# Metaformer on one NeuronCore: 87 of 4608 gathered rows are fetched by SyncE, position by position

## The chip, the cores and the metric

The kernel runs on one core of a Trainium2 chip. The metric is the device time of one execution in microseconds (us), lower is better. The engines are named as the profile names them: PE is TensorE (PEld its weight loads), DVE is VectorE, ACT is ScalarE, POOL is GpSimd, and SP is SyncE, which computes nothing and issues most of the DMAs. SPq stands for SyncE's queue.

## The reference

Four images of 128 channels and 128 x 128 pixels pass two layers. What matters here is the first one, a deformable 3 x 3 convolution. For each pixel and each of the nine taps, an offset is computed by an ordinary convolution, and the image is sampled bilinearly at the shifted place:

```python
g = jax.vmap(lambda img, yy, xx: img[:, yy, xx])(x, iyc, ixc)
return g * (w * valid.astype(x.dtype))[:, None]
...
return corner(y0, x0, wy0 * wx0) + corner(y0, x1, wy0 * wx1) + corner(y1, x0, wy1 * wx0) + corner(y1, x1, wy1 * wx1)
```

`x` is the image after a normalisation over its channels. The samples are weighted with `w_conv` and summed over the taps. After it come, for each pixel, a mixture of the two best of eight experts, a channel mixing that equals the reference's Fourier layer, and a layer of 64 experts that takes eight tokens each from an image.

## The kernel before, in words

**The table.** For each image the kernel writes a table into the device memory (`Image.table`): for each pixel of the padded image the 128 normalised channels of the pixel and of the one below it, 256 float32. Two neighbouring entries, 2 KB, hold the four corners of a sample. `positions` computes for each pixel and tap the entry's number (`Image.index`, one per partition, where the partition is the pixel's column x) and the four corner weights (`Image.weight`).

**Chunks.** A group is four image rows (`row_groups`), and a `Chunk` is one tap of a group: 4 rows x 128 pixels. There are 32 groups x 9 taps x 4 images = 1152 chunks. `Chunk.gather` issues one indirect DMA on GpSimd for each of the four rows; it brings 128 entries of 2 KB onto 128 partitions, into the tile `g` (six buffers, `AHEAD`). `weighted` multiplies three of the rows by their corner weights on VectorE in one instruction (all four rows for tap 0), `weighted_too` does the fourth on ScalarE with four activations, `summed` adds the four corners by 16 accumulating transposes on TensorE into `trg`, and `moved` copies the result to `sT` on ScalarE. `Group.convolved` multiplies `sT` with the convolution's weights into `sums`, and `mixed` does what follows for the group (experts, mixing, gates).

**The order.** A loop over `n` at the end of the kernel walks the chunks. Each chunk has two half steps ("slots"); `Turns` holds jobs (Python generators) that are resumed in those slots, so that the work of other stages is laid between the chunks. The order in which the loop records instructions is the order on each engine (`InOrder`, the helper whose line the profile shows as L104 for nearly everything). After `summed` of chunk n, the gathers of chunk n + 6 are issued. The table and positions of image b + 1 are made by jobs during the chunks of image b: `block` (transposes, normalisation, the store of the table), `padding` (a transpose and a copy into one of four buffers `pads`), `offsets` (six matmuls on two padded buffers), `positions`.

**SyncE's queue** holds the loads and stores in the order of recording: `xc` (image rows), `table<-ent` (the table's blocks), `xg` (the residual's rows of a group), `x_d<-x` (the group's result), and from the fourth image on the expert weights and the output of the first three images. A DMA's waits hold back all that stands behind it on the queue.

**Memory.** From the fourth image on, buffers that are no longer needed take expert weights: `rooms` lists among others `flat_pads`, the four padded buffers. `blank` is a block of zeros that a matmul with `iota` uses to clear `sums`.

Of the kernel before, what the change touches and what calls it, by code (L numbers as in the profile page):

```python
# [42 lines left out]
F32 = mybir.dt.float32  # L43
I32 = mybir.dt.int32
U32 = mybir.dt.uint32
AF = mybir.ActivationFunctionType
ALU = mybir.AluOpType
AX = mybir.AxisListType
# [3 lines left out]
P = 128  # L52
# [5 lines left out]
HID = 512  # L58
# [6 lines left out]
TAPS = 9  # L65
EPS_C = 1e-6
EPS_T = 1e-5
RB = 8
CB = 16
TW = P + 1  # L70
TC = P + 2
# [14 lines left out]
BANKS = 6  # L86
AFTER = 11
SPACE = 13
BLOCK = 84
FILL = "fill"  # L90
DONE = "done"
# [98 lines left out]
def metaformer_kernel(  # L190
# [50 lines left out]
    with ExitStack() as main:  # L241
# [91 lines left out]
        for pad in pads:  # L333
            nc.vector.memset(pad, 0.0)
        flat_pads = [pad.rearrange("p y x -> p (y x)")[:, 0:HID].unsqueeze(1) for pad in pads]
        aT_sb = wts.tile([P, P], F32, name="aT_sb")

        gwT_sb = wts.tile([P, 2 * E1], F32, name="gwT_sb")
        gb_sb = wts.tile([P, 1], F32, name="gb_sb")


        blank = wts.tile([P, P], F32, name="blank")
        nc.vector.memset(blank, 0.0)
        flip = wts.tile([P, P], F32, name="flip")
        nc.gpsimd.memset(flip, 0.0)
        for base in (0, -P):
# [108 lines left out]
                yield from with_bias(ew_sb[:, 4 * h : 4 * h + 4, :], biases[h])  # L455


        def padding(t, h, row, read, padded):

            yield FILL  # L460
            tr = transposes(row, 4)
            read.append(h)
            yield turns.hop
            eng.scalar.copy(pads[(2 * t + h) % 4][:, :, 1 : P + 1], tr)
            padded.append(h)

        def offsets(im, t, padded):

            while len(padded) < 2:
                yield 1  # L470
            yield 1


            yield FILL
            po = bank([P, 4, P], "po")
            for k in range(3):
                for h in range(2):
                    eng.tensor.matmul(
                        po[h * P // 2 : (h + 1) * P // 2],
                        lhsT=woff_sb[:, k, :],  # L480
                        rhs=pads[(2 * t + h) % 4][:, :, k : k + P],
                        start=(k == 0),
                        stop=(k == 2),
                    )
            yield turns.hop
# [13 lines left out]
            yield turns.hop  # L499
            if i0 == 0:  # L500
                im.z[q] = pa.tile([P, CB + 2, 6 * TAPS], F32, name=f"z{im.b}_{q}", tag="z")
                if q == 0:
                    eng.vector.memset(im.z[q][:, 0, :], 0.0)
                else:
                    eng.scalar.copy(im.z[q - 1][:, CB + 1, :], tr[:, 0, 0, 0 : 6 * TAPS])
            eng.scalar.copy(
                im.z[q][:, 1 + i0 : 1 + i0 + RB, :].rearrange("p (h i) o -> p h i o", h=2),
                tr[:, :, :, 0 : 6 * TAPS].rearrange("p i h o -> p h i o"),
            )
            if i0 == 0 and q > 0:  # L510
# [192 lines left out]
        class Group:  # L703
# [30 lines left out]
            def convolved(self, k):  # L734

                yield 1
                if k + 1 < FIRST:
                    return
                if k + 1 == FIRST:
                    eng.tensor.matmul(  # L740
                        sums.rearrange("p s c -> p (s c)"),
                        lhsT=blank,
                        rhs=iota,
                        start=True,
                        stop=False,
                    )
# [13 lines left out]
                if k + 1 == TAPS:  # L760
                    yield turns.hop
                    yield from mixed(self)

        class Chunk:


            def __init__(self, group, k):
                self.group, self.k = group, k
                self.shared = k > 0

            def gather(self):
                self.g = pg.tile([P, 4, 4, P], F32, name="g", tag="g")
                im = self.group.im
                for s, y in enumerate(self.group.rows):
                    eng.gpsimd.indirect_dma_start(
                        out=self.g[:, s].rearrange("p v c -> p (v c)"),
                        out_offset=None,
                        in_=im.table,
                        in_offset=bass.IndirectOffsetOnAxis(
                            ap=im.index[:, y, self.k : self.k + 1], axis=0  # L780
                        ),
                    )

            def weighted(self):
                n = 3 if self.shared else 4
# [4 lines left out]
                )  # L790

            def weighted_too(self):
                g, y = self.g[:, 3], self.group.rows[3]
                w = self.group.im.weight[y // CB]
                for v in range(4):
                    eng.scalar.activation(
                        g[:, v, :], g[:, v, :], AF.Copy, scale=w[:, y % CB, self.k, v : v + 1]
                    )

            def summed(self):  # L800

                self.tr = bank([P, 4, P], "trg")
                for s in range(4):
                    for v in range(4):
                        eng.tensor.matmul(
                            self.tr[:, s, :],
                            lhsT=self.g[:, s, v, :],
                            rhs=ident,
                            is_transpose=True,
                            start=(v == 0),  # L810
                            stop=(v == 3),
                        )

            def moved(self):
# [2 lines left out]
                eng.scalar.copy(group.sT[self.k], self.tr)  # L817
                turns.start(group.convolved(self.k))


        exps = []

# [766 lines left out]

        def in_turn():  # L1590

            for b in range(NB):
                for number, (rows_of, minus, runs) in enumerate(orders[b]):
                    im = images[b]
                    if im.sent <= P // RB or not im.weight.keys() >= {y // CB for y in rows_of}:
                        raise ValueError("a table is late")
                    group = Group(images[b], number, rows_of, minus, runs)
                    group.begin()
                    for k in range(TAPS):
                        chunk = Chunk(group, k)  # L1600
                        chunk.gather()
                        yield chunk

        source = in_turn()
        chunk = [next(source) for _ in range(AHEAD)]
        turns.hop = HOP
# [5 lines left out]
        def tick(more):  # L1612

            turns.fills(0)
            turns.slot += 1
            if more and total - QUICK <= n <= total:
                turns.steps()
                turns.fills(0)
                turns.slot += 1

        while n < total + 3 or turns.jobs:
# [134 lines left out]
```

## Time and profile before

| | |
|---|---|
| median of 14 runs | 6119.08 us (6113.19 to 6127.06) |
| the profiled execution | 6122.13 us, of which the trace's span is 6120.4 us |
| granted clock of TensorE, mean | 0.96 |
| first and last gather start | 119.9 us and 5927.3 us |
| busy: PE, PEld, DVE, ACT, POOL | 5442.7, 4446.7, 4842.3, 3819.6, 4467.1 us |
| DMA: mean rate; share of GpSimd's queue, of SyncE's and ScalarE's | 249 GB/s; 64.7%, 14.2% |
| DMAs of SyncE | 687 |

Busy time counts what an engine executes; registers, waits and the issuing of DMAs on SyncE are not counted. A gather on GpSimd counts as busy while GpSimd makes its descriptors. In a line of the timeline stand the start in us from the span's start, the duration in us, the engine, the source line, the operation, the tile written and the tiles read, the count, and in brackets the idle time before it with what ended it. In a line of the waits stand the total in us, how often, and the longest.

### The profile page before, as it was taken

The page shows a single profiled execution, that of the slowest core. Times are in us where ns is not written, and L with a number is a line of the kernel's source. Part 1 is how long each engine was busy: PE and PEld are TensorE (multiplying, and loading weights), DVE is VectorE, ACT ScalarE, POOL GpSimd, SP SyncE. Part 2 cuts the span into 40 slices and gives each one's busy share as a digit, 9 for nine tenths or more (in the row PEclk, how much of TensorE's full clock was granted, in tenths as well). Part 3 has the DMA queues.
Part 4 walks back from the last instruction along what each step waited for, and adds up shares of the span by engine and source line. Part 5 has one row for each costly group of instructions (what it writes and reads, how often), then busy time and mean ns, then how long its engine had stood idle before and what let it go on. Part 6 is the DMA issues. An engine that isn't in the chain of part 4 may idle for free.

```text
span 6120.4 us, 118020 instructions
## 1 busy us (share of the span) xinstructions
PE 5442.7 (89%) x38823; PEld 4446.7 (73%) x38823; DVE 4842.3 (79%) x15420; ACT 3819.6 (62%) x9910; POOL 4467.1 (73%) x4795
## 2 busy tenths in 40 slices
PE   6899999998899999989889999999888898999984
PEld 4777777777777777777777777777677687777763
DVE  5678888887788888888778888888788787888872
ACT  4567666665666666666666666666555565666652
POOL 5777777777777777777777777777777777777750
PEclk8999999999999999999999999999999999999997
DMA  7778787877777877877777777778777897998777
GB/s 235 227 238 257 240 254 243 253 236 224 240 242 241 248 241 246 250 234 225 231 246 245 242 242 248 238 245 249 222 225 215 293 339 218 323 337 312 225 226 277
DMA packets 579234, 1526.15 MB, mean 249 GB/s; under 512 B 86456, under 2 KB 225408, under 8 KB 578624
## 3 DMA queue, kind: packets, MB, share of 16 engines
q0 software_dynamic: 369664, 1210.35, 64.7%
q1 hardware_dynamic: 206656, 299.87, 14.2%
q8 instruction: 310, 5.08, 0.3%
q10 hardware_dynamic: 2304, 8.39, 0.3%
q14 instruction: 300, 2.46, 0.1%
HBM read 1381.43 MB, written 136.85 MB: 248 GB/s over the span
## 4 chain that ended last, share of the span: by engine, by line
PE 33%; DMA 25%; DVE 15%; ACT 10%; POOL 9%; issue 8%; DVEq 0%; POOLq 0%; ACTq 0%; SPq 0%
DMA g<-table,index 22%; PE trg L104 11%; PE sums L104 9%; POOL g L104 9%; PE pe L104 6%; DVE g L104 6%; DVE x L104 4%; ACT g L104 4%; PE po L104 2%; DMA out<-w 2%; PE tr L104 2%; ACT sT L104 1%; ACT xn L104 1%; ACT L104 1%; PE small L104 1%
## 5 line engine op out<-in xcount | busy, mean ns | idle before, releaser
L104 POOL DMA_INDIRECT g<-table,index x4608 | 4367.8, 948 | 1416.1 <-issue 984.2
L104 DVE TENSOR_TENSOR g<-g,small 128x1536 f32<-128x1536 f32 (+1 forms) x1152 | 2081.8, 1808 | 881.2 <-DMA g<-table,index 762.0
L104 PE MATMUL trg<-ident,g 128*128 128x128 f32 x18432 | 2274.8, 278 | 158.4 <-DVE g L104 61.2
L104 PEld LDWEIGHTS trg<-ident,g 128*128 128x128 f32 x18432 | 2108.5, 144 | 279.4 <-DVE g L104 66.8
L104 ACT ACTIVATE g<-g,weight 128x128 f32<-128x128 f32 x4096 | 1306.1, 391 | 813.2 <-DMA g<-table,index 804.6
L104 DVE SCALAR_TENSOR_TENSOR x<-pe,gate,x 128x128 f32<-128x128 f32 x4072 | 1384.2, 341 | 102.2 <-PE pe L104 49.1
L104 PEld LDWEIGHTS sums<-wconv_sb,sT 128*128 128x128 f32 x9216 | 1139.1, 194 | 339.6 <-ACT sT L104 185.0
L104 PE MATMUL sums<-wconv_sb,sT 128*128 128x128 f32 x9216 | 1214.1, 280 | 139.1 <-ACT sT L104 138.2
L104 PE MATMUL pe<-ew_sb,nT 128*128 128x512 f32 x2048 | 1053.3, 613 | 168.7 <-ACT sT L104 145.2
L104 ACT COPY sT<-trg 128x512 f32<-128x512 f32 x1152 | 653.4, 568 | 115.3 <-PE trg L104 114.9
L104 PEld LDWEIGHTS pe<-ew_sb,nT 128*128 128x128 f32 x2048 | 332.3, 195 | 340.2 <-ACT sT L104 197.7
L104 ACT ACT_TABLE_LOAD x263 | 337.4, 1283 | 7.5 <-DVE nmax L104 2.2
L104 ACT ACTIVATE xn<-x,c_nb,c_rs 128x128 f32<-128x128 f32 x512 | 211.3, 485 | 163.0 <-DVE c_nb L104 163.0
L104 ACT ACTIVATE n<-x,b_nb,b_rs 128x128 f32<-128x128 f32 x512 | 210.3, 482 | 131.1 <-DVE b_nb L104 64.3
L104 ACT ACTIVATE c_rs<-c_mv,eps_c 128x4 f32<-128x4 f32 x128 | 37.9, 296 | 401.9 <-DVE c_mv L104 398.7
L104 ACT ACTIVATE tn<-x,d_nb,d_rs 128x128 f32<-128x128 f32 x512 | 210.9, 483 | 73.8 <-DVE d_nb L104 73.8
L104 PE MATMUL po<-pad,woff_sb 128*64 128x512 f32 x768 | 193.7, 623 | 24.0 <-DVE x L104 21.0
L104 PEld LDWEIGHTS sums<-ident,xg 128*128 128x128 f32 x1024 | 147.9, 208 | 74.0 <-issue 74.0
L104 ACT ACTIVATE ent<-raw,a_nb,a_rs 128x128 f32<-128x128 f32 x384 | 157.9, 484 | 15.9 <-DVE a_nb L104 14.0
L104 PEld LDWEIGHTS ps<-aT_sb,xfT 128*128 128x128 f32 x1024 | 131.5, 199 | 46.3 <-ACT xfT L104 38.1
L104 PE MATMUL ps<-aT_sb,xfT 128*128 128x128 f32 x1024 | 143.9, 285 | 20.8 <-ACT xfT L104 20.1
L104 PE MATMUL sums<-iota,blank 128*128 128x512 f32 x256 | 151.8, 679 | 0.0
(236 smaller groups left out, 5108.5 us busy)
## 6 DMA issues: line engine op xcount, KB each, us to landing
g<-table,index POOLq DMA_INDIRECT x4608, 3.8
table<-ent SPq DMA_DIRECT2D x48, 1024.0 KB, 6.4
xc<-in_x SPq DMA_DIRECT2D x64, 512.0 KB, 8.8
w<-x_d SPq DMA_DIRECT2D x64, 512.0 KB, 6.2
xg<-in_x SPq DMA_DIRECT2D x124, 256.0 KB, 6.9
x_d<-x SPq DMA_DIRECT2D x124, 256.0 KB, 4.2
out<-w SPq DMA_DIRECT2D x48, 512.0 KB, 7.0
w<-in_weight SPq DMA_DIRECT2D x42, 512.0 KB, 7.6
```

The costliest lines, as they stand in the source:

```text
L104: return self.tc.keep_in_program_order(issue(*args, **kwargs))
```

## The change

One row in each thirteen chunks is no longer gathered by GpSimd. `Lone` picks chunks (never tap 0) in advance, one after the other, and has the fourth row of each fetched by SyncE: 128 DMAs of 2 KB, one for each position, whose source address comes from a register. To get there, VectorE multiplies the row's 128 entry numbers by 1024 (bytes), TensorE transposes them onto one partition into a free corner of the PSUM tile `small`, VectorE copies them as integers to a place in SBUF, and SyncE loads 16 of them at a time into registers. Five DMAs are recorded in each half step, 26 half steps for a row; the next row follows at once. 87 rows are taken this way in the whole kernel. The chunk that uses a row stands so that nine half steps lie between the row's last DMAs and its use. `weighted_too` and `summed` then read the fetched row in place of the fourth part of `g`.

The rows land in two of the four padded buffers (`apart`). So `padding` and `offsets` use only the other two once the main loop runs, with a flag `busy` for each, and in `rooms` two spare tiles of the weights' pool stand in for these two buffers. `blank` is dropped for a part of `zeros`.

```diff
+RUN = 13
...
+        apart = [
+            pad.rearrange("p y x -> p (y x)")[:, 0:HID].rearrange("p (v c) -> p v c", c=P)
+            for pad in pads[2:]
+        ]
+        busy = [False, False]
+        lined = wts.tile([1, P], I32, name="lined")
...
-        blank = wts.tile([P, P], F32, name="blank")
-        nc.vector.memset(blank, 0.0)
...
+        def pad_of(t, h):
+            return pads[(2 * t + h) % 4 if turns.hop == 1 else h]
+
         def padding(t, h, row, read, padded):
 
+            while turns.hop > 1 and busy[h]:
+                yield 1
+            busy[h] = True
             yield FILL
...
-            eng.scalar.copy(pads[(2 * t + h) % 4][:, :, 1 : P + 1], tr)
+            eng.scalar.copy(pad_of(t, h)[:, :, 1 : P + 1], tr)
...
-                        lhsT=blank,
+                        lhsT=zeros[:, 0:P],
...
             def gather(self):
                 self.g = pg.tile([P, 4, 4, P], F32, name="g", tag="g")
                 im = self.group.im
                 for s, y in enumerate(self.group.rows):
+                    if s == 3 and self.lone is not None:
+                        continue
                     eng.gpsimd.indirect_dma_start(
...
+        class Lone:
...
+            def look(self, t):
+
+                i, begin = len(self.users), max(t + 16, self.end)
+                n = (begin + 2 * RUN + 9) // 2 + 1
+                n += n % TAPS == 0
...
+                self.users.append(n)
+                self.tiles[n] = apart[i % 2]
+                self.end = begin + 2 * RUN
+                self.ahead = self.job(i, n, im, im.index[:, y, k : k + 1], begin)
+
+            def job(self, i, n, im, index, begin):
+                places, scaled = self.places[i % 2], bx_i.bitcast(F32)[:, i % 2, 0:1]
+                eng.vector.tensor_scalar(scaled, index, 8.0 * P, None, ALU.mult)
+                yield
+                yield
+                eng.tensor.transpose(small[0:1, HID - P : HID], scaled, ident)
+                yield
+                eng.vector.tensor_copy(places, small[0:1, HID - P : HID])
+                while self.now < begin:
+                    yield
...
+                for p in range(P):
+                    if p % 16 == 0:
+                        loads, values = nc.values_load_multi_w_load_instructions(
+                            places[:, p : p + 16],
+                            engines=[mybir.EngineType.SP],
...
+                    eng.sync.dma_start(
+                        out=apart[i % 2][p : p + 1]
+                        .rearrange("p (h v) c -> p h (v c)", h=2)
+                        .bitcast(U8),
+                        in_=flat[bass.ds(values[p % 16], 16 * P)]
+                        .rearrange("(o h c) -> o h c", o=1, h=2),
+                    )
+                    if p % (P // (2 * RUN) + 1) == P // (2 * RUN):
+                        yield
...
                         chunk = Chunk(group, k)
+                        chunk.lone = lone.tiles.get(n)
+                        n += 1
                         chunk.gather()
...
                 chunk[n].summed()
                 turns.fill()
+                lone.turn(2 * n)
...
             turns.steps()
+            if 0 <= n < total:
+                lone.turn(2 * n + 1)
...
-                rooms = [[part(), part()], [part(), part()], flat_pads]
+                rooms = [[part(), part()], [part(), part()], flat_pads[0:2]]
+                rooms[-1] += [spare(), spare()]
```

More of the change, by code (lines that the diff above doesn't have):

```diff
@@ L45 @@
 U32 = mybir.dt.uint32
+U8 = mybir.dt.uint8
 AF = mybir.ActivationFunctionType
@@ L480, in offsets @@
                         lhsT=woff_sb[:, k, :],
-                        rhs=pads[(2 * t + h) % 4][:, :, k : k + P],
+                        rhs=pad_of(t, h)[:, :, k : k + P],
                         start=(k == 0),
@@ L484, in offsets @@
                     )
+            busy[:] = [False, False]
             yield turns.hop
@@ L769, in __init__ @@
                 self.shared = k > 0
+                self.lone = None
             def gather(self):
@@ L782, in gather, with last @@
                     )
+            def last(self):
+                return self.g[:, 3] if self.lone is None else self.lone
             def weighted(self):
@@ L792, in weighted_too @@
             def weighted_too(self):
-                g, y = self.g[:, 3], self.group.rows[3]
+                g, y = self.last(), self.group.rows[3]
                 w = self.group.im.weight[y // CB]
@@ L803, in summed @@
                 for s in range(4):
+                    g = self.g[:, s] if s < 3 else self.last()
                     for v in range(4):
@@ L806, in summed @@
                             self.tr[:, s, :],
-                            lhsT=self.g[:, s, v, :],
+                            lhsT=g[:, v, :],
                             rhs=ident,
@@ L818, in moved, with __init__, turn @@
                 turns.start(group.convolved(self.k))
+        class Lone:
+            def __init__(self):
+                self.places = [lined, by_i.rearrange("p y a b -> p (y a b)")[0:1, 0:P]]
+                self.tiles, self.users, self.end = {}, [], 0
+                self.ahead = self.filling = None
+                self.values = []
+            def look(self, t):
+                i, begin = len(self.users), max(t + 16, self.end)
+                n = (begin + 2 * RUN + 9) // 2 + 1
+                n += n % TAPS == 0
+                b, k = divmod(n, slots)
+                number, k = divmod(k, TAPS)
+                if n >= total or b not in images or i > 1 and begin <= 2 * self.users[-2]:
+                    return
+                im, y = images[b], orders[b][number][0][3]
+                if im.sent <= P // RB or im.known <= y // CB:
+                    return
+                self.users.append(n)
[12 more added lines that the diff above has]
+                    yield
+                self.filling, self.ahead = self.ahead, None
+                flat = im.table.rearrange("e c -> (e c)").bitcast(U8)
+                values = []
+                for p in range(P):
[3 more added lines that the diff above has]
+                            engines=[mybir.EngineType.SP],
+                            min_val=0,
+                            max_val=8 * P * (TW * TC - 2),
+                            skip_runtime_bounds_check_because="positions are clamped to the table",
+                        )
+                        for load in loads:
+                            tc.keep_in_program_order(load)
+                    eng.sync.dma_start(
[4 more added lines that the diff above has]
+                        .rearrange("(o h c) -> o h c", o=1, h=2),
+                    )
+                    if p % (P // (2 * RUN) + 1) == P // (2 * RUN):
+                        yield
+                if self.now >= 2 * n - 2:
+                    raise ValueError("a row is late")
+            def turn(self, t):
+                self.now = t
+                if self.filling is not None and next(self.filling, DONE) is DONE:
+                    self.filling = None
+                if self.ahead is None:
+                    self.look(t)
+                if self.ahead is not None:
+                    next(self.ahead)
@@ L1590, in in_turn @@
         def in_turn():
+            n = 0
             for b in range(NB):
@@ L1600, in in_turn @@
                         chunk = Chunk(group, k)
+                        chunk.lone = lone.tiles.get(n)
+                        n += 1
                         chunk.gather()
                         yield chunk
+        lone = Lone()
         source = in_turn()
@@ L1653, in metaformer_kernel @@
                 part = lambda: late.tile([P, 2, HID], F32, name="w", tag="w", bufs=4)
-                rooms = [[part(), part()], [part(), part()], flat_pads]
+                spare = lambda: pw.tile(
+                    [P, 1, HID], F32, name="w", tag="weight", bufs=3 * P // CB // 2
+                )
+                rooms = [[part(), part()], [part(), part()], flat_pads[0:2]]
+                rooms[-1] += [spare(), spare()]
                 rooms.append([pw.tile([P, 2, HID], F32, name="w", tag="index")])
```

## The prediction

> **What bounds the kernel now.** I read the page first (busy times, then the costliest groups), then GpSimd's timeline, the waits, the busy times by stage, and last the SyncE queue's timeline and the tile views. The page, part 1 and the first line of part 5:
>
> ```profile
> PE 5442.7 (89%) x38823; PEld 4446.7 (73%) x38823; DVE 4842.3 (79%) x15420; ACT 3819.6 (62%) x9910; POOL 4467.1 (73%) x4795
> ...
> L104 POOL DMA_INDIRECT g<-table,index x4608 | 4367.8, 948 | 1416.1 <-issue 984.2
> ```
>
> By busy share TensorE looks like the bound and GpSimd (POOL) looks a quarter idle. The group's line says otherwise: busy and idle time together are 5783.9 us for 4608 gathers, 1.255 us each, and most of that idle time waits for nothing that the profile shows. GpSimd's timeline in mid-kernel:
>
> ```profile
> 2998.30 0.95 POOL L104 DMA_INDIRECT g<-table,index  x1 [0.30 <-issue]
> 2999.55 0.95 POOL L104 DMA_INDIRECT g<-table,index  x1 [0.30 <-issue]
> 3000.80 0.94 POOL L104 DMA_INDIRECT g<-table,index  x1 [0.30 <-PE pe L104]
> 3002.05 0.95 POOL L104 DMA_INDIRECT g<-table,index  x1 [0.30 <-DMA g<-table,index]
> ```
>
> The starts stand 1.25 us apart, whatever releaser is named: 0.95 us of work and 0.30 us before the next one. GpSimd issues gathers without a break, four to a chunk, so a chunk takes 5.02 us. The consumers wait for it:
>
> ```profile
> ACT g L104 <- DMA g<-table,index: 804.6, 448, 19.2
> DVE g L104 <- DMA g<-table,index: 762.0, 455, 14.7
> ```
>
> And the busy times by stage (PE, PEld, DVE, ACT, POOL) show who is next:
>
> ```profile
> 300.00:4400.00 4100.00, 3739.86 (x26268) 3061.17 (x26267) 3363.39 (x10892) 2703.62 (x7056) 3102.61 (x3275) 0.97 0.79 242
> 4400.00:5930.00 1530.00, 1379.27 (x10209) 1152.78 (x10209) 1228.62 (x3600) 916.48 (x2368) 1153.63 (x1217) 0.96 0.83 271
> ```
>
> 3275 gathers in 4100 us is 1.252 us each: the gathers set this stage. TensorE is busy 91% of it, VectorE 82%.
>
> **Part one, what is removed.** 87 of 4608 gathers leave GpSimd: 87 x 1.255 = 109 us. They come out of the bound, nearly evenly (one in each 13 chunks, 1131 chunks of 1152), so all of it can be had if nothing else sets the pace. TensorE would then stand at about 91% x 5784 / 5675 = 93%, still below its limit. The profiled execution took 6122.13 us (its span is 6120.4), 3 us above the median of the runs. The gain alone gives 6122 - 109 = 6013.
>
> **Part two, what is added on SyncE.** Each of the 87 rows becomes 128 DMAs of 2 KB, which is 11136 DMAs on a queue that issued 687, and eight register loads of 16 positions. The order of the changed program shows 87 x 8 = 696 such loads, no other new work between the DMAs, and one of eight completion semaphores, in rotation, that each DMA waits for: the DMA eight places before must have landed. The rows follow each other without a gap, so SyncE must do a row, and all that it did before, in the time of 13 chunks. That is 52 x 1.255 = 65.3 us at the pace of before and 51 x 1.255 = 64.0 us with the gain. This budget decides. What one DMA costs on SyncE is read in its timeline, first near 338 us, then near 56 us and 5994 us:
>
> ```profile
> 337.37 0.37 SPq L104 DMA_DIRECT2D x_d<-x  x1
> 337.79 1.14 SPq L104 DMA_DIRECT2D table<-zeros  x2
> 338.97 0.96 SPq L104 DMA_DIRECT2D xc<-in_x  x2
> ...
> 55.65 0.53 SPq L104 DMA_DIRECT2D gb_sb<-in_gate_b  x1
> 56.23 0.58 SPq L104 DMA_DIRECT2D gwT_sb<-in_gate_w  x1
> ...
> 5993.84 5.83 SPq L104 DMA_DIRECT2D w<-in_weight  x9
> ```
>
> A DMA that stands alone takes 0.33 to 0.37 us. DMAs back to back take more: the pair of table<-zeros 1.14 us, or 0.57 each, the xc pair 0.48 each, start to start about 0.05 more. The pair of zeros is the nearest row, because its second DMA is the only 2 KB transfer of two 1 KB pieces in this kernel; the tile view gives that one 0.62 us (461 is its larger partner):
>
> ```profile
> L104 SPq DMA_DIRECT2D table<-zeros x2: 461/542/624, 337.8 to 338.3; - x2
> ```
>
> So the issue is bounded by 0.33 + 0.05 = 0.38 us and 0.62 + 0.05 = 0.67 us. The second bound on a DMA is its landing, as eight are in flight: the fastest landing in the views of SyncE's loads and stores is 3.1 us, the gathers' median 3.8, the table's zeros 5.6, so 0.39, 0.48 or 0.70 us for each.
>
> ```profile
> g<-table,index POOLq DMA_INDIRECT x4608, 3.8
> DMA to landing us min/median/max: 3.1/4.3/7.3
> ```
>
> (The second line is from the tile view of x_d.) I take 0.55 us a DMA: above the 0.48 of large DMAs back to back, below the 0.67 of the same shape, because part of that one's time may come from the 256 KB transfer just ahead of it. A register address was never used on this queue; it can add and hardly save. Of a register load no row exists. Bounds are nothing and, if it took as long as the fastest landing, 3.1 us; I take 0.5, one more instruction of the size of an isolated or a back-to-back DMA. SyncE's other DMAs between the first and the last gather are 549 in 1152 chunks, 6.2 in 13 chunks, at 0.45 us.
>
> A row: 128 x 0.55 + 8 x 0.5 + 6.2 x 0.45 = 70.4 + 4.0 + 2.8 = 77.2 us, against 65.3. SyncE becomes the bound and each row costs 11.9 us: 87 x 11.9 = +1035 us, and GpSimd's 109 us are lost in its new idle time. 6122 + 1035 = 7157 in the profile's terms, 7155 by the median.
>
> The Trainium skill bears on the one price that has no row. "Runtime: NRT & Kernel Launch", section "Instruction fetch mechanics", puts such a register load at about 200 ns for each register, even in bulk. That would be an estimate of 8 x 16 x 0.2 = 25.6 us a row in place of 4.0, and about 9035 us in all; "DMA: Bandwidth & Descriptors", section "Latency and other measured facts", has only a floor of some 600 ns for a load, with which nothing changes. No run here shows which it is.
>
> The landings above are 3.1 us and more, for transfers of 192 KB and up. "DMA: Bandwidth & Descriptors", section "Anatomy of one DMA — SWDGE (gpsimd) path", has a fit with a fixed part near 2.0 us for a DMA issued by GpSimd; with that for a small DMA of SyncE, eight in flight would allow 0.25 us each, and the limit would vanish behind the issue. No row of this trace shows a landing so short.
>
> **Part three, the small edits.** A row's indices cost one VectorE scaling, one 128x128 TensorE transpose and one copy: 87 x about 0.17 us (the timeline's reciprocal of four columns), 87 x 0.28 (the mean of the trg transposes) and 87 x at most 0.3 (a statistics instruction on 128x128 takes 0.29), 25 us for TensorE and 41 for VectorE, beside 9% and 18% idle time; without that cover the price would be at most 65 us. The clearing matmul reads another block of zeros: same size, no cost. Two buffers instead of four for the padded rows serialise a pair with its offset matmuls; the pairs come some 13 or more half chunks apart, so I price it at nothing, and at one ACT copy of 0.6 us a pair if not covered (64 pairs, 38 us). Behind SyncE's new waits stand its table stores, x_d stores, image loads and xg loads; they are asked for a group or more ahead of their use (a group is 45 us), so lateness of a few us is harmless, and a row itself has nine half chunks, 22 us, between its last DMA and ScalarE's scaling. A queue that is overloaded on the average uses this up in the second row. The fetched row's consumer is the same four ACT operations as before; they, and TensorE's transposes behind them, are who waits.
>
> **The rivals.**
> 1. *SyncE keeps up and GpSimd's gain arrives.* One condition: a position costs less than (64.0 - 4.0 - 2.8) / 128 = 0.447 us. For it speak the 0.33 us of isolated DMAs, and only two descriptors instead of 128 behind each; against it, every back-to-back row above. Time: 6013, faster by 1.8%.
> 2. *Landing decides, and with a long latency.* The 2 KB DMAs sit on the same queue behind 512 KB and 1 MB transfers and beside gathers that hold the DMA engines 79% busy. At 5.6 us, 0.70 us each: 89.6 + 4.0 + 2.8 = 96.4 us a row, 6122 + 87 x 31.1 = 8828.
> 3. *Nothing moves.* SyncE needs just about 65 us, or TensorE at 93% with its bursts takes over what GpSimd gives. Time: about 6119.
>
> **How the numbers follow.** SyncE bound by issue: 0.50. Its own range goes from 0.48 us a DMA (68.2 us a row, 6375) to 0.67 (92.6 us, 8497). Landing decides: 0.14, above that. The gain arrives: 0.32, from 6005 (the runs of before scatter by 6 to 8 us) to 6100. Nothing moves: 0.04. The range that holds 8 in 10 must span both sides and leaves out only the 0.14: 6005 to 8500. What a measurement of this kernel can tell from no change is about 0.2%, 12 us; so faster 0.32, same 0.04, slower 0.64.
>
> **What the profile after will show.** If the forecast is right, SyncE's timeline is one unbroken run of pad<-table DMAs with starts 0.5 us or more apart; GpSimd's gathers, 4521 of them, keep 0.95 us but show idle time for free g buffers; ScalarE waits for DMA pad<-table; and TensorE's busy share falls to some 76%. If rival 1 is right, SyncE shows gaps at its other waits, gathers still start every 1.25 us, and ACT's waits name g, not pad. If rival 2 is right, SyncE's DMAs are short (below 0.45 us) with waits for DMA pad<-table between them, and landings stand above 5 us. A DMA on SyncE below 0.44 us with its share of the register loads would make the prediction wrong.

## The result, and the profile after

The change makes the kernel slower, by much less than predicted. The median is 6201.99 us (6195.76 to 6207.91) against 6118.99 us: +83.0 us, a ratio of 1.0136, interval 1.0126 to 1.0146. Predicted was 7155 us, so the direction came out as forecast and the size was more than twelve times too large. The profiled execution took 6197.98 us (its span is 6196.2), 75.9 us more than that of before.

The page after, first line of part 1 and first line of part 5. The helper that records the instructions now stands at L106:

```profile
PE 5476.3 (88%) x38910; PEld 4463.3 (72%) x38910; DVE 4855.6 (78%) x15593; ACT 3814.7 (62%) x9910; POOL 4386.0 (71%) x4708
...
L106 POOL DMA_INDIRECT g<-table,index x4521 | 4287.3, 948 | 1568.9 <-issue 1066.9
```

The 87 gathers have left GpSimd and a gather still takes 948 ns, but its idle time has grown from 1416.1 to 1568.9 us. 152.8 us more idle less 80.5 us less busy is about the whole loss. The waits of the whole kernel name the same releasers as before, and shorter:

```profile
ACT g L106 <- DMA g<-table,index: 578.1, 324, 19.2
DVE g L106 <- DMA g<-table,index: 556.2, 358, 14.8
```

ScalarE waited 804.6 us for gathers and now 578.1. No wait for `DMA pad<-table` is among the long ones: the fetched rows themselves are hardly ever waited for. GpSimd's timeline in mid-kernel shows the old period of 1.25 us:

```profile
2998.23 0.95 POOL L106 DMA_INDIRECT g<-table,index  x1 [0.30 <-issue]
2999.48 0.95 POOL L106 DMA_INDIRECT g<-table,index  x1 [0.30 <-DVE a_mv L106]
3000.74 0.95 POOL L106 DMA_INDIRECT g<-table,index  x1 [0.31 <-issue]
```

So mid-kernel the bound is where it was, with fewer gathers in it. Where the loss lies shows when the same chunks are compared in both traces. The start of a chunk is here the start of VectorE's weighting of it, in us; the last two columns are two experiments that follow below, as differences to the same kernel before.

| chunk | before | after | difference | half pace | quarter transfers |
|---|---|---|---|---|---|
| 0 | 128 | 128 | +0.3 | -0.2 | +0.5 |
| 480 | 2534 | 2491 | -43.1 | -44.8 | -44.3 |
| 864 | 4459 | 4379 | -80.7 | -82.0 | -80.5 |
| 912 | 4713 | 4631 | -82.0 | -84.6 | -81.0 |
| 960 | 4956 | 4898 | -57.7 | -85.9 | -84.4 |
| 1008 | 5213 | 5205 | -8.1 | -80.7 | -80.1 |
| 1056 | 5454 | 5506 | +51.4 | -82.0 | -72.2 |
| 1104 | 5703 | 5780 | +77.8 | -92.8 | -75.1 |
| 1151 | 5931 | 6006 | +74.8 | -93.6 | -77.7 |

Two kernels in one. Up to chunk 864, 65 of the rows bring 80.7 us, 1.24 us each, as GpSimd's period says. Between chunks 912 and 1104, 159.8 us are lost, and after that nothing. The windows of before and of after for those stages (columns: window, length; busy time and count of PE, PEld, DVE, ACT, POOL; granted clock, DMA share, GB/s), before first:

```profile
4713.00:5703.00 990.00, 907.23 (x6948) 759.35 (x6947) 789.17 (x2302) 599.41 (x1541) 744.34 (x786) 0.97 0.88 298
```

```profile
300.00:4380.00 4080.00, 3770.69 (x26717) 3095.51 (x26716) 3417.57 (x11139) 2731.13 (x7142) 3087.23 (x3257) 0.98 0.80 246
4631.00:5780.00 1149.00, 961.89 (x6964) 787.34 (x6962) 790.65 (x2329) 599.37 (x1540) 729.62 (x771) 0.92 0.79 256
```

The same 192 chunks took 990 us and now 1149. VectorE, ScalarE and GpSimd do the same work in both (789 and 791, 599 and 599, 744 and 730 us), the DMA engines' share even falls, 0.88 to 0.79. Only TensorE is busy for longer, 962 us for 907, at a granted clock of 0.92 for 0.97, but over a smaller share of the stretch (84% for 92%). So something waits.

SyncE is what has changed. The tile view of `pad` and the view of the line that loads registers (columns: count, duration min/median/max in ns, first and last start in us, number of forms):

```profile
L106 SPq MOVE pad<-table x11136: 29/29/43, 140.2 to 5952.7; - x199
L106 SPq DMA_DIRECT2D pad<-table x11136: 217/228/1518, 140.3 to 5952.7; - x199
```

```profile
L883 SPq TENSOR_LOAD <-lined x352: 1147/1237/3923, 138.9 to 5943.2; - x176
L883 SPq TENSOR_LOAD <-by_i x344: 1137/1238/4092, 201.6 to 5888.4; - x172
```

A position costs 0.228 us of DMA and 0.029 of a register move; the median from start to start is 0.323 us. Sixteen registers cost 1.24 us. SyncE's timeline in the third image (start, duration, x count of a run; register loads aren't shown in it):

```profile
3006.05 20.15 SPq L106 DMA_DIRECT2D pad<-table  x40
3026.41 0.41 SPq L106 DMA_DIRECT2D xg<-in_x  x1
3026.92 6.14 SPq L106 DMA_DIRECT2D pad<-table  x15
3033.24 0.39 SPq L106 DMA_DIRECT2D x_d<-x  x1
```

Forty positions in 20.15 us are 0.50 us each, with register loads and waits in between. Added up over rows from the trace, in us for one row from its start to the next one's (positions: their DMAs, moves and the gaps below 0.15 us; waits: all longer gaps; two of the lines are of experiments that follow below):

| rows | positions | loads | other DMAs | waits | a row | budget |
|---|---|---|---|---|---|---|
| forecast | 70.4 | 4.0 | 2.8 | 0 | 77.2 | 65.3 |
| after, rows 5 to 61 | 44.3 | 10.9 | 1.9 | 6.7 | 63.9 | 64.0 |
| twelve chunks a row, rows 10 to 64 | 44.3 | 10.5 | 1.7 | 5.3 | 61.8 | 60.2 |
| after, rows 71 to 82 | 44.7 | 10.8 | 6.6 | 19.1 | 81.4 | 67.0 |
| quarter transfers, rows 71 to 82 | 44.0 | 10.2 | 6.8 | 7.9 | 69.1 | 67.0 |

In the first three images SyncE keeps step with the chunks, and issues a row's last DMA 21 us before its use on the average (rows 5 to 61). The budget of 64.0 us is 51 gathers, the pace with the gain; 60.2 is 48 gathers, the pace of before, and the budget of the rows 71 to 82 is the pace of before in that stage, 990 / 192 x 13 = 67.0 us.

SyncE's waits (total, times, longest) in the first three images, then in the stretch that loses:

```profile
SPq L106 <- DMA pad<-table: 117.2, 326, 1.2
SPq L106 <- DMA xc<-in_x: 80.2, 47, 3.5
SPq L106 <- DMA xg<-in_x: 64.1, 60, 2.3
SPq L106 <- DMA x_d<-x: 49.7, 50, 2.3
SPq L106 <- DMA table<-ent: 35.6, 28, 3.2
```

```profile
SPq L106 <- DMA w<-in_weight: 82.5, 55, 3.7
SPq L106 <- DMA w<-x_d: 76.5, 44, 3.9
SPq L106 <- DMA out<-w: 25.0, 23, 2.3
SPq L106 <- DMA pad<-table: 21.9, 64, 0.9
```

In the kernel before, SyncE waited in that stretch mostly for engines, for these two longest:

```profile
SPq L104 <- DVE x L104: 227.0, 8, 47.7
SPq L104 <- PE pf L104: 165.9, 17, 33.9
```

Added up over the whole view, SyncE waited there for engines in 726 of the 990 us. In the change it waits for engines in 45 of the 1149 us, and for landings in 234. Slower engines, TensorE with its lower clock included, would show as waits of SyncE for them; it is SyncE that now sets the pace of this stretch.

In the fourth image SyncE also loads the expert weights and `x_d` for the output of the first three images, and stores that output: 16.5 other DMAs a row (rows 71 to 82), where there were 4.6. By the table a row takes 17.5 us more than in the first three images: 4.7 for issuing those DMAs and 12.4 in waits, and the fence of the stretch that loses names their landings. Two of them in SyncE's timeline:

```profile
5209.69 0.35 SPq L106 DMA_DIRECT2D w<-x_d  x1
5210.15 4.00 SPq L106 DMA_DIRECT2D pad<-table  x5
5214.24 0.35 SPq L106 DMA_DIRECT2D w<-x_d  x1
5214.70 7.23 SPq L106 DMA_DIRECT2D pad<-table  x13
```

The last thirteen positions take 7.23 us, where 0.323 us each would be 4.2, and no register load lies among them. In the trace two of the thirteen wait, 1.5 and 1.6 us, for the landings of the two `w<-x_d` above. The fetched rows themselves are hardly late: the last DMA of the rows 71 to 73 is issued 2 to 3 us before its use, but that of the rows 75 to 82 11 to 24 us. It is what stands among them that comes late. Who waits for the late queue in that stretch (after):

```profile
POOL g L106 <- issue: 238.5, 560, 10.0
ACT w L106 <- DMA out<-w: 125.1, 25, 7.8
DVE w L106 <- DMA out<-w: 69.2, 16, 8.1
```

ScalarE and VectorE stand in front of `w` tiles whose store has not landed (ScalarE's wait of this kind was 42.0 us in the kernel before), the chunks recorded behind run late, and GpSimd issues its gathers late: its `issue` time was 170.5 us in the same stage of before. No single wait carries the loss. In the chain of waits from 4600 to 5700 us SyncE's work stands in many places: `w<-in_weight` 8.0%, `w<-x_d` 7.9%, `pad<-table` 7.4%, SyncE's own issuing 6.7%, `out<-w` 6.6%.

### The profile page after: what moved, and what is told of

It reads as the page before. It is cut to its first block, busy times and chain, and to the rows that moved or that the text cites. A ratio compares the mean times of both kernels' runs of the same rounds, so it can differ in the third digit from the quotient of the medians.

```text
span 6196.2 us, 141180 instructions
## 1 busy us (share of the span) xinstructions
PE 5476.3 (88%) x38910; PEld 4463.3 (72%) x38910; DVE 4855.6 (78%) x15593; ACT 3814.7 (62%) x9910; POOL 4386.0 (71%) x4708
## 4 chain that ended last, share of the span: by engine, by line
PE 31%; DMA 24%; DVE 17%; ACT 9%; issue 8%; POOL 7%; SPq 3%; DVEq 0%; ACTq 0%; POOLq 0%
DMA g<-table,index 16%; PE trg L106 10%; PE sums L106 9%; POOL g L106 7%; DVE g L106 6%; PE pe L106 6%; DVE x L106 4%; ACT g L106 3%; SPq L106 2%; PE po L106 2%; DMA pad<-table 2%; DMA w<-in_weight 2%; PE tr L106 2%; DMA w<-x_d 2%; DMA out<-w 1%
## 5 line engine op out<-in xcount | busy, mean ns | idle before, releaser
L106 POOL DMA_INDIRECT g<-table,index x4521 | 4287.3, 948 | 1568.9 <-issue 1066.9
L106 DVE TENSOR_TENSOR g<-g,small 128x1536 f32<-128x1536 f32 (+1 forms) x1152 | 2081.6, 1808 | 791.8 <-DMA g<-table,index 556.2
L106 PE MATMUL trg<-ident,g 128*128 128x128 f32 x18084 | 2229.1, 278 | 134.0 <-DVE g L106 45.2
L106 PEld LDWEIGHTS trg<-ident,g 128*128 128x128 f32 x18084 | 2070.7, 144 | 245.4 <-issue 86.2
L106 ACT ACTIVATE g<-g,weight 128x128 f32<-128x128 f32 x3748 | 1194.7, 391 | 622.5 <-DMA g<-table,index 578.1
L106 DVE SCALAR_TENSOR_TENSOR x<-pe,gate,x 128x128 f32<-128x128 f32 x4072 | 1383.7, 341 | 128.4 <-PE pe L106 76.2
L106 PEld LDWEIGHTS sums<-wconv_sb,sT 128*128 128x128 f32 x9216 | 1143.5, 195 | 296.5 <-issue 149.8
L106 PE MATMUL sums<-wconv_sb,sT 128*128 128x128 f32 x9216 | 1216.4, 280 | 96.3 <-ACT sT L106 95.5
L106 PE MATMUL pe<-ew_sb,nT 128*128 128x512 f32 x2048 | 1051.5, 612 | 149.7 <-ACT sT L106 95.2
L106 ACT COPY sT<-trg 128x512 f32<-128x512 f32 x1152 | 652.8, 568 | 136.2 <-PE trg L106 135.3
L106 PEld LDWEIGHTS pe<-ew_sb,nT 128*128 128x128 f32 x2048 | 331.2, 194 | 317.9 <-ACT sT L106 133.3
L106 ACT ACTIVATE xn<-x,c_nb,c_rs 128x128 f32<-128x128 f32 x512 | 211.2, 485 | 156.2 <-DVE c_nb L106 156.0
L106 ACT ACTIVATE n<-x,b_nb,b_rs 128x128 f32<-128x128 f32 x512 | 210.3, 482 | 120.2 <-DVE b_nb L106 60.6
L106 ACT ACTIVATE c_rs<-c_mv,eps_c 128x4 f32<-128x4 f32 x128 | 37.9, 296 | 391.7 <-DVE c_mv L106 376.6
L106 ACT ACTIVATE tn<-x,d_nb,d_rs 128x128 f32<-128x128 f32 x512 | 210.9, 483 | 80.0 <-DVE d_nb L106 79.7
L106 PEld LDWEIGHTS sums<-ident,xg 128*128 128x128 f32 x1024 | 148.5, 209 | 73.3 <-issue 66.1
L106 PE MATMUL po<-pad,woff_sb 128*64 128x512 f32 x768 | 190.5, 613 | 8.5 <-ACT sT L106 4.7
L106 ACT COPY w<-pf 128x512 f32<-128x512 f32 x64 | 37.1, 585 | 222.7 <-DMA out<-w 131.8
L106 ACT ACTIVATE ent<-raw,a_nb,a_rs 128x128 f32<-128x128 f32 x384 | 158.0, 484 | 20.1 <-DVE a_nb L106 18.4
L106 PEld LDWEIGHTS ps<-aT_sb,xfT 128*128 128x128 f32 x1024 | 132.0, 200 | 48.4 <-ACT xfT L106 33.8
L106 PE MATMUL ps<-aT_sb,xfT 128*128 128x128 f32 x1024 | 145.2, 287 | 24.5 <-ACT xfT L106 18.0
```

Source lines behind the costliest of these rows:

```text
L106: return self.tc.keep_in_program_order(issue(*args, **kwargs))
```

## The experiments

Three theories for the 160 us lost in the fourth image: **Q**, SyncE's queue falls behind there; **D**, the 2 KB transfers disturb the DMA engines; **R**, the buffers that the fetched rows took away from the expert weights (`rooms`, `pads`) cost it. The time before in these comparisons is 6117.61 us for the first four, 6120.28 for the next four, and 6119.02 for the last three.

**No rows in the fourth image.** 65 rows instead of 87, all memory edits kept.

```diff
-                if n >= total or b not in images or ...
+                if n >= LATE * slots or b not in images or ...
```

> The change with fetched rows only for chunks of the first three images: 65 rows instead of 87, every other edit kept (two spare tiles in rooms, two padded buffers instead of four). Theory Q (in the fourth image SyncE also issues expert weights and output tiles, its queue overflows, and what stands behind it comes late): the fourth image costs again what it cost before, and 65 x 1.255 = 82 us of gathers are gained: 6037 us. Rival R (it is the memory edits, the spare tiles and the two padded buffers that are missing, which delay the expert weights): the fourth image stays about 155 us longer than before, 6190 us. Rival D (the 2 KB transfers hold up the large ones on the DMA engines): 6037 us too; another run tells it from Q.

6043.16 us, ratio 0.9877 (0.9860 to 0.9893). The 74 us won in three images stay, so R falls: with the same buffers and no fetches there is no loss. Each row is worth 74.5 / 65 = 1.15 us.

**A pause only in the busy stretch.** 73 rows.

```diff
+                if 2 * 905 <= begin < 2 * 1085:
+                    return
```

> The change with no fetch begun in chunks 905 to 1085, where the trace of the change shows 10 to 26 other DMAs of SyncE beside each row: 73 rows. Theory Q and rival D: 73 x 1.255 = 92 us gained, 6027 us. Rival R: about 6180 us. If the rows at both ends of the fourth image cost something as well, it comes out slower than 6037 us, the time expected of the kernel without any row in the fourth image.

6038.10 us, 0.9869 (0.9853 to 0.9886), 11 us above the number expected, and about the 6043.16 us of the kernel without rows in the fourth image: the eight rows before and after the stretch cost nothing that can be measured.

**128 bytes a position.** All 87 rows and all their DMAs, a sixteenth of the data.

```diff
-                        out=apart[i % 2][p : p + 1]
-                        .rearrange("p (h v) c -> p h (v c)", h=2)
-                        .bitcast(U8),
-                        in_=flat[bass.ds(values[p % 16], 16 * P)]
-                        .rearrange("(o h c) -> o h c", o=1, h=2),
+                        out=apart[i % 2][p : p + 1].rearrange("p v c -> p (v c)").bitcast(U8)[:, 0:P],
+                        in_=flat[bass.ds(values[p % 16], P)].unsqueeze(0),
```

> The change with all 87 rows and all 11136 DMAs, but each brings 128 bytes instead of 2 KB (the rest of a fetched row is left out). SyncE issues as many instructions as in the change, the DMA engines move 21 MB less. Theory Q (issue time on SyncE): same time as the change, 6190 to 6205 us. Rival D (2 KB pieces on the DMA engines delay gathers and large transfers): most of the loss of the fourth image goes, 6030 to 6080 us.

6190.17 us, 1.0118 (1.0101 to 1.0135). Only 12 us of the 83 go with the bytes, so D is not the cause. A DMA costs SyncE as much as before:

```profile
L106 SPq DMA_DIRECT2D pad<-table x11136: 218/228/1610, 141.0 to 5939.3; - x199
```

SyncE's waits in the stretch are what they were (86.1 us for `w<-x_d`, 80.9 for `w<-in_weight`). What is left is Q: the number of DMAs on SyncE, or the waits among them.

**Two pieces for each position.** To test the price that the prediction used: rows only in the first three images, each position written as two pieces of 1 KB with a gap between them, as the store of zeros was.

```diff
-            pad.rearrange("p y x -> p (y x)")[:, 0:HID].rearrange("p (v c) -> p v c", c=P)
+            pad.rearrange("p y x -> p (y x)").rearrange("p (h w) -> p h w", h=2)[:, :, 0 : 2 * P]
...
-                        out=apart[i % 2][p : p + 1]
-                        .rearrange("p (h v) c -> p h (v c)", h=2)
-                        .bitcast(U8),
+                        out=apart[i % 2][p : p + 1].bitcast(U8),
```

> As the kernel without rows in the fourth image, but each position lands as two pieces of 1 KB with a gap between them, the shape of the 2 KB store of zeros whose 0.62 us the prediction leaned on. If that shape itself is dear, a DMA takes about 0.6 us on SyncE, a row 128 x 0.6 + 10.4 + 2.8 = 90 us, and the time is 6119 + 65 x (90 - 65) = about 7730 us. If the 0.62 us came from the 256 KB transfer ahead of it, a DMA takes 0.23 to 0.30 us and the time stays near 6037 us.

8448.65 us in the one run, 719 us above the number expected, with SyncE the bound. The tile view of `pad` and two lines of the waits:

```profile
L106 SPq DMA_DIRECT2D pad<-table x8320: 523/562/1685, 140.0 to 6764.0; - x199
```

```profile
DVE lined L106 <- SPq L885: 1126.4, 30, 46.8
ACT pad L106 <- DMA pad<-table: 890.4, 59, 55.0
```

The same 2 KB in two pieces takes 0.562 us, 0.657 from start to start, close to the prediction's upper end of 0.67. In the change the two halves lie next to each other on both sides, and they travel as one piece: the page of after has 22272 more packets on SyncE's queue than before, two for each position, and this kernel 33280, four for each. At chunk 864 it stands 2331.8 us behind the kernel before, 35.9 us a row over 65.3, so a row costs 101 us. Expected were 90, with 0.6 us for a position. This is what a SyncE-bound change looks like: VectorE waits 1126.4 us to overwrite a row's indices (`lined`) that SyncE hasn't yet loaded.

**Twelve chunks a row, with the pause.** How far is the row from its budget in the first three images?

```diff
-RUN = 13
+RUN = 12
```

> As the kernel with the pause in the busy stretch, but a row in twelve chunks instead of thirteen: 80 rows. Theory Q prices a row on SyncE, by the trace of the change in its first three images, at 128 x 0.323 + 8 x 1.30 + 1.7 for other DMAs + about 5 of waits for landings = 58.4 us, against a budget of 47 x 1.255 = 59.0 us: it just fits, 80 rows gain about as much each as the 73 did (79.5 us measured, 1.09 a row), 6030 us. If waits for landings grow when rows stand closer, the queue is over-full in all images and the time rises above 6117 us.

6197.43 us, 1.0128 (1.0111 to 1.0145): a miss. From row 10 to 64 the rows start 61.8 us apart, over the budget of 60.2, and their last DMAs are issued 3.4 us before their use, on the average, where the change has 21. So a row that nothing holds back takes not 58.4 but 61.8 us (the table above has its parts), and thirteen chunks leave it some 2 us to spare.

**Eleven chunks a row, first three images only.**

```diff
-RUN = 13
+RUN = 11
...
-                if n >= total or b not in images or ...
+                if n >= LATE * slots or b not in images or ...
```

> As the kernel without rows in the fourth image, but a row in eleven chunks: 77 rows. Theory Q: a row needs 57.9 us of SyncE and has 43 x 1.255 = 54.0 us; SyncE is the bound in the first three images, each row costs 57.9 - 44 x 1.255 = 2.7 us, and the time is 6117 + 77 x 2.7 = 6325 us. If SyncE had room to spare there, 77 rows would gain 84 us: 6033 us.

6521.39 us, 1.0654 (1.0636 to 1.0671). Rows start 61.1 us apart (rows 10 to 64). The budget at the pace of before is 11 x 5.02 = 55.2 us. 77 rows x 5.9 = 454 us, less some 50 us that the first rows have in hand (the first is issued 54 us before its use, the sixth 2 us), is about 404, and at chunk 864 the trace has +418. So the prediction's rule, rows times what a row costs over its budget, holds once SyncE is the bound, with 61 us for a row. The expected 6325 came from 58.4. The wait that shows it is the one from the two-piece kernel:

```profile
DVE lined L106 <- SPq L883: 321.2, 32, 15.2
DVE by_i L106 <- SPq L883: 301.7, 32, 15.2
```

**Half the pace in the busy stretch.** 79 rows, those of the stretch over 26 chunks each.

```diff
-                n = (begin + 2 * RUN + 9) // 2 + 1
+                run = 26 if 2 * 892 <= begin < 2 * 1085 else RUN
+                n = (begin + 2 * run + 9) // 2 + 1
...
-                    if p % (P // (2 * RUN) + 1) == P // (2 * RUN):
+                    if p % (P // (2 * run) + 1) == P // (2 * run):
```

> The change, but rows that begin in chunks 892 to 1085 are spread over 26 chunks instead of 13: 79 rows. Theory Q: half the positions per chunk leave SyncE room for its other DMAs, nothing comes late, 79 rows gain 86 us: 6031 us. If any fetch in that stretch does harm (through the waits on shared completion semaphores), it stays above 6060 us.

6032.56 us, 0.9861 (0.9845 to 0.9878), as expected, and the best version that was run: it beats both kernels. The table above has its chunks: the gain is kept through the stretch and grows.

**Output stores on ScalarE's queue.** Two ways to read Q: the output stores are late because they stand behind fetches (**Qa**), or the fetches wait for the landings of large DMAs (**Qb**). Each DMA of SyncE uses one of eight completion semaphores in rotation (in the trace of the change all but 9 of 11815 DMAs take the one of the DMA eight places ahead), so a fetch can't be issued before that DMA has landed. All 222 waits for a landing that SyncE's view counts in the stretch are for this semaphore. Eight fetches are issued in 2.6 us, the large loads landed in 5.9 to 13.5 us in the trace of before.

```diff
-                    (eng.sync if self.among else eng.scalar).dma_start(
+                    eng.scalar.dma_start(
```

> The change with all 87 rows, but the 48 stores out<-w of the first three images' output are issued by ScalarE instead of SyncE. Sub-theory Qa (the loss comes from output stores and loads that stand behind fetches on SyncE's queue, so that buffers come free late and the engines that wait for them in order stand still): much of the 155 us lost in the fourth image returns, 6090 to 6150 us. Sub-theory Qb (SyncE is held up by the landings of large transfers and the fetched rows come late): no change, about 6195 us.

6208.55 us, 1.0145 (1.0128 to 1.0162). Nothing is won. With these stores off its queue SyncE still waits 90.8 us for `w<-x_d` and 83.4 for `w<-in_weight` in the stretch, and its rows still take about 80 us. The waits of ScalarE and VectorE for `out<-w` fall there to 25.3 and 2.7 us, but ScalarE has new ones:

```profile
ACT tn L106 <- DMA pad<-table: 31.4, 4, 10.1
ACT g L106 <- DMA pad<-table: 28.8, 6, 9.0
```

Added up, ScalarE's waits for landings of `pad<-table` are 142 us in the stretch, where the change has 14. ScalarE's stores take their turn in the same eight semaphores, so before a store ScalarE waits for the fetch eight places ahead. The run moves a wait to ScalarE instead of removing one: it doesn't support Qa, and doesn't exclude it.

**Fetched and gathered.** The first experiment with the gathers left in: 65 rows are fetched, and GpSimd gathers them too.

```diff
-                    if s == 3 and self.lone is not None:
-                        continue
```

> As the kernel without rows in the fourth image (65 rows, 6043 us), but GpSimd gathers those rows as well, so that nothing is taken off it. If the gain of that kernel is GpSimd's relief and the fetches cost nothing while SyncE keeps up, the time is that of before, 6115 to 6125 us. If some of the gain came from other edits, it stays below 6110 us; if the fetches themselves slow the gathers, it rises above 6130 us.

6121.06 us, 1.0004 (0.9994 to 1.0013). The fetches, the index transposes, the copies and the buffer edits together cost nothing measurable while SyncE keeps up; the gain is GpSimd's alone.

**A quarter of the large transfers.** Both kernels with the fourth image's expert weights, `x_d` loads and output stores cut to a quarter of their bytes, as many DMAs as before. The cut is the same in both; its main lines:

```diff
-                        eng.sync.dma_start(out=room, in_=src[:, e : e + n, :])
+                        c = P if self.quarter else HID
+                        eng.sync.dma_start(out=room[:, :, 0:c], in_=src[:, e : e + n, 0:c])
...
+                    c = P if self.among else HID
...
-                        out=xt.rearrange("p i c -> p (i c)"),
+                        out=xt[:, :, 0:c],
```

The kernel before with the cut:

> The kernel before, with the expert weights of the first three images' pass, and the loads and stores of their output tiles, cut to a quarter of their bytes (the rest of those weights and tiles is left out; the number of DMAs is the same). It is the base for the next run: 6060 to 6119 us, since some waits for these transfers go.

6116.32 us, 0.9992 (0.9983 to 1.0002): the large transfers cost the kernel before nothing that can be measured.

The change with the cut:

> The change with all 87 rows and the same cut to a quarter as the run before it. Sub-theory Qb (in the fourth image SyncE's fetches wait for the landing of the large transfers with which they share eight completion semaphores): these landings become short, SyncE keeps its thirteen chunks a row, and the time is about 87 x 1.09 = 95 us below that of the run before it. Sub-theory Qc (the number of SyncE's instructions in that stretch is too large, whatever their bytes): it stays 60 to 85 us above it.

6048.63 us, 0.9883 (0.9866 to 0.9899): 67.7 us faster than the kernel before with the same cut, where the change with whole transfers is 83 slower. SyncE's waits in the stretch, of this kernel:

```profile
SPq L106 <- DMA w<-x_d: 22.6, 27, 1.4
SPq L106 <- DMA w<-in_weight: 19.4, 24, 1.9
SPq L106 <- DMA pad<-table: 18.1, 54, 1.3
```

With the same number of DMAs, the waits for `w<-x_d` fall from about 75 to 22.6 us and those for `w<-in_weight` from 82.5 to 19.4, and a row there takes 69.1 us instead of 81.4, nearly all of the difference in the column of waits (7.9 for 19.1). So most of the lateness comes from the length of the landings, as Qb has it, and not from the count of instructions. Of the 95 us expected 68 came: with 6.8 us for its other DMAs a row of the stretch still misses its budget by 2 us, so these rows bring nothing and cost a little. Between chunks 912 and 1104 this kernel takes 995 us and its own base, the kernel before with the same cut, 978: of the 160 us lost there 17 are left.

What stays open: the cut shortens the transfers on the rings as well as their hold on the semaphores, so these two are not separated, and no run shows how much of the loss reaches the engines through the output stores (Qa). A kernel with more completion semaphores wasn't tried, as the language layer rotates through its eight.

## Why the prediction was wrong, by its steps

**The bound and the gain: right.** GpSimd's gathers at 1.255 us set the pace; 65 rows brought 1.24 us each by chunk 864, and 1.09 to 1.15 us each in the whole time of the three versions that keep the gain. TensorE, at 92% of the first three images, took nothing back.

**One position on SyncE: the step that failed.** The prediction bounded it by 0.38 and 0.67 us and took 0.55, near the store of zeros, as "the only 2 KB transfer of two 1 KB pieces". It measured 0.323 us from start to start (0.346 in the mean), below even the lower bound, which came from DMAs to 128 partitions, although a register move of 0.029 us that the prediction didn't have stands before each. The row was of the wrong shape: a position is one piece, and with two pieces the same position does cost 0.657 us. Over a row this is 44.3 us in place of 70.4, 26 us too much, and the forecast's whole excess was 11.9. Rival 1's condition, a position below 0.447 us, was met. With the measured prices the forecast's own sum is 44.3 + 10.5 + 2.8 = 57.6 us a row, inside the 64.0, and its rule then gives rival 1's 6013 us. So that the change came out slower, as forecast, is luck: the loss comes from waits that this sum doesn't have, in a sixth of the kernel.

**A register load: too small.** 1.24 us in place of 0.5, and 10.5 us a row in place of 4.0; within the bounds of nothing and 3.1. The Trainium skill's figure in "Runtime: NRT & Kernel Launch", section "Instruction fetch mechanics" (200 ns a register; by the page's terms these are loads from HBM) is not what this trace shows for positions that lie in SBUF: 1.24 us for sixteen are 77 ns each. By the page's figure eight loads would be 25.6 us a row, an estimate that is 15 us above what was measured.

**Landing: the mechanism was right, the place and the releaser were not.** Rival 2 charged every position with its own landing. For the fetches themselves this hardly counts: `pad<-table` costs SyncE 117.2 us in the first three images, 1.8 us a row, so most land before the eighth next one is issued, within some 2.6 us. The estimate that the prediction took from "DMA: Bandwidth & Descriptors", section "Anatomy of one DMA — SWDGE (gpsimd) path", for a small DMA, near 2.0 us, is not contradicted by that. What counts is the landing of the large DMAs that share the queue. The forecast's sum had no wait for them; SyncE's waits are 5 to 7 us a row in three images and 19.1 in rows 71 to 82.

**SyncE's other DMAs: averaged over stages that differ.** 6.2 in 13 chunks was the mean over the kernel; it is 4.6 in rows 5 to 61 and 16.5 in rows 71 to 82. With their landings, this is what turned a row of 62 us, inside the budget, into one of 81. The trace of before holds the counts by stage: 314 DMAs in the 864 chunks of three images, 4.7 in thirteen, and 216 in the 192 chunks of the stretch, 14.6 in thirteen. The prediction didn't take them.

**What a backlog costs: right where there was one.** The test is the kernel with eleven chunks a row: 404 us by the rule, 418 in the trace. In the stretch of the change 13 chunks took 67.0 us before and 1149 / 192 x 13 = 77.8 us, 10.8 us over; that is the measured loss put in rows and no test of its own. (The 81.4 of the table is the mean of the twelve rows in its middle.) The prediction applied the same rule, rows times excess, to all 87 rows.

**The small edits: right.** They were priced at nothing, and the run that fetched and gathered 65 rows stands 2 us above the kernel before, and the interval of its ratio holds 1.

**The signs named in advance.** Gathers still start every 1.25 us and ScalarE's waits name `g`, not `pad`: rival 1's signs, in three images. SyncE's DMAs are short with waits between them: rival 2's sign, in the fourth, where the releasers are the expert weights and `x_d`. Of the forecast's own signs, `pad` in ScalarE's long waits appears where SyncE sets the pace in three images, with twelve chunks a row (240.3 us), eleven (208.0) and two pieces (890.4), and TensorE far below 88% in the two-piece kernel alone (66%). The time is the sum of the two rivals, each in its stage, a case that the prediction didn't have: a gain of about 82 us, then a loss of 160.

## What to carry to other kernels

Price a DMA's issue from a row of the same shape, counted in pieces after neighbours are merged and not as the source writes them, and look for that shape in the program's order before choosing a row. Where work is spread evenly over a kernel, make the budget for each stage and not for the mean: here three quarters of the kernel had 2 us to spare per row, and a sixth of it lacked 11. Short DMAs behind long ones on one queue wait for the long ones' landings when they share a few completion semaphores, so slow down or pause the short ones where the long ones run: half the pace in a sixth of the kernel turned +1.4% into -1.4%. In this program the stores of ScalarE take their turn in the same eight semaphores as SyncE's DMAs, so moving a store to that engine moved the wait with it.

## What the runs showed of the hardware that was not expected

- A 2 KB DMA from a register address costs SyncE 0.228 us as one piece and 0.562 as two; a sixteenth of the bytes in one piece changed the kernel's time by 12 us of 6200. A DMA of 128 bytes costs SyncE the same 0.228 us. On this queue the pieces cost, hardly the bytes.
- A load of sixteen registers from SBUF takes 1.24 us, at least 1.14, and 1.49 in the kernel with two pieces.
- 11136 more DMAs on SyncE's queue, 22.8 MB in all, left the period of GpSimd's gathers at 1.25 us in the three images where SyncE kept up.
- The granted clock of TensorE was lower where TensorE waited: 0.97 at 92% busy and 0.92 at 84% in the stretch before and after, 0.829 over the whole two-piece kernel at 66%. No run separates which follows which.
